# Counting sixteen of 128 edge tiles ahead of the first projection of a graph network, with one-hots from GpSimd and ScalarE

## The chip, the cores and the metric

The kernel runs on one core of a Trainium2 chip. The metric is the device time of one execution in microseconds (us), the median of several runs. Engine names are those of the profile: PE is TensorE's matmul, PEld its weight load, DVE is VectorE, ACT is ScalarE, POOL is GpSimd, SP is SyncE, which here only issues DMAs.

## What is computed

A graph network over 1024 nodes of 512 features and 16384 edges. The rows of x are normalised and cut at zero, normalised again over the nodes (a batch norm), and go through a graph convolution; four layers of cross attention and a gated feed-forward follow, and a second graph convolution. Cut to what matters here:

```python
h = max(layernorm(x), 0)
h = batchnorm(h) ; h = gcn(h, src, dst, gcn_in_w)
for i in range(4): h += attention(ln(h), cond) ; h += feed_forward(ln(h))
h = gcn(h, src, dst, gcn_out_w) ; return x + h + h0
# gcn: out[d] = sum over edges (s, d) of (h @ W)[s] * dinv[s] * dinv[d] + b, with self loops
```

A graph convolution is done as a product with a dense matrix of counts: how many edges run from source s to target d. The change concerns how that matrix is built, once, in the opening of the kernel. The targets are sorted.

## The kernel before

**Order.** The kernel is written as one program. A scheduler places each engine's instructions by their dependencies and by the order of the program text; `tc.issue_after(x)` keeps what is issued under it behind x in that order, and `waiting_for(x, engine)` (L82) makes each instruction of one engine wait for x. Each engine works its own queue strictly in order.

**The opening, to 27 us.** SP and ACT issue the loads of the edges (L333, L334), of x in eight blocks (L338), of two groups of `cond`, and of weights. POOL makes the identity, issues seven small loads of parameters (`prow`, `grow`, L356 to L362), casts the identity to bf16 (L484) and numbers the nodes 0 to 1023 in f32 (`ids_f`, L346). DVE splits each edge's source into a low part (0 to 127) and a high part and combines the high part with the target's offset in its window into one key (L370 to L383). PE turns both so that an edge tile is a column (L393), ACT copies them out (`edges_t`, L401; `minus_low`, L404), then PE turns the parameters (`pc`, `pg`, L397 and L399) and ACT copies those (L409, L410). ACT also casts the numbers to f16 (`ids`, L411). PE turns four blocks of `cond` (L184 `tr_cond`, copied by ACT at L244), then the eight blocks of x that DVE has normalised (statistics L151 and L152, root L134 to L143, scaling L172; transposes L184 `tr_x`; ACT cuts at zero into `h0T`, L431). DVE takes the batch statistics of `h0T` (L437, L439), works out the root and the scale and shift (L134 to L143, L443 to L445, the last being `bshift`), and DVE and ACT apply them (L450, L453). Meanwhile PE turns four more blocks of `cond` and makes the first key products (`pa_kT`, L301), in two halves with an ACT copy between (`firsts`, L322).

**The counting loop, 27 to 79 us.** The 16384 edges are 128 tiles of 128 edges. Because the targets are sorted, a tile's edges fall in a window of 48 targets (`WIN`). For tile t, `count(t)` makes two one-hot matrices, `low` (edge by low part, 128x128) and `hot` (edge by high part and window offset, 128x384), and PE multiplies them into PSUM (`cs`, L537); a finished half block gets the identity added (L534), is copied by ACT (L541), and is summed by DVE into degrees (`degrees`, L491). `hot` is always made by DVE (L524). `low` is made by DVE for four tiles of each eight (L502), and by ACT for the other four (`low_hots`, L505: four Abs, one Relu). Into this loop the 32 steps of the first projection (`hw_in`, L461, a step being one 128x512 product that the profile records as two matmuls) are woven, one for each four tiles (L626 to L629), by a generator. `low` has 5 buffers, `hot` 10, `off` 2. PSUM has 8 banks in turn (`bank`, L92).

**After it**: the first value product, the last degrees, a branch for unsorted inputs that is not taken (L637), the root of the degrees, the aggregation (L655), and the four layers.

Of the kernel before, what the change touches and what calls it, by code (L numbers as in the profile page):

```python
# [10 lines left out]
BF16 = mybir.dt.bfloat16  # L11
F32R = mybir.dt.float32r
I32 = mybir.dt.int32
AF = mybir.ActivationFunctionType
OP = mybir.AluOpType
AX = mybir.AxisListType

P = 128
# [5 lines left out]
def gnn_kernel(  # L24
# [26 lines left out]
    nc = tc.nc  # L51

    N, D = x.shape
# [6 lines left out]
    NB = N // P  # L60
    KC = D // P
    HP = H // 2
    ET = E // P
# [17 lines left out]
    @contextmanager  # L81
    def waiting_for(ins, engine):  # L82

        traced = nc.cur_bb.bb.instructions
        n = len(traced)
        yield
        for i in traced[n:]:
            if i.engine == engine:
                tc.add_manual_dep(i, ins.ins.name, mybir.DependencyInfo(
                    mybir.DependencyClass.Sync, mybir.DependencyReason.DATA))  # L90

    def bank(name):  # L92
        return psum.tile([P, 512], F32, tag="bank", name=name)

    def t512(name, dtype=F32):
        return work.tile([P, 512], dtype, tag="t512", name=name)

    def slot(name):
        return slots.tile([P, 2, 512], F32, tag="slot", name=name)

    def slots_of(n, name):
        return [slot(f"{name}_{i}") for i in range(n)]
# [17 lines left out]
    def four(t):  # L120
        return t.rearrange("p (a b) -> p a b", a=4)
# [67 lines left out]
    ident = const.tile([P, P], F32, name="ident")  # L189
    make_identity(nc, ident)  # L190
    ones = const.tile([P, 1], F32, name="ones")
# [40 lines left out]
    def turn_cond(g, by=(0, 1)):  # L232

        t = slots_of(4, f"ct_0_{g}")
        tiles = raw_conds.pop(g)
        for i, ctile in enumerate(tiles):
            pt = transposed(ctile, f"cond_{g}_{i}")
            r0 = (i % MB) * P
            to = t[i // MB].rearrange("p a (b c) -> p a b c", b=2)[:, :, :, r0:r0 + P]
            of = pt.rearrange("p (a b c) -> p a b c", a=2, b=2)  # L240
            if by[i % 2]:
                nc.vector.tensor_copy(to, of)
            else:
                nc.scalar.copy(to, of)  # L244
        return t
# [91 lines left out]
    for nb in range(NB):  # L337
# [4 lines left out]
    w_in = load_w(gcn_in_w, "w_in")  # L342
    raw_wv = load_w(Wv[0], "wv_0")

    ids_f = slot("ids_f").rearrange("p a b -> p (a b)")
    numbered = nc.gpsimd.iota(ids_f, pattern=[[1, N]], base=0, channel_multiplier=0,  # L346
                   allow_small_or_imprecise_dtypes=True)
    ids = gp.tile([P, N], F16, name="ids")
    tid = gp.tile([P, 1], I32, name="tid")
    nc.gpsimd.iota(tid, pattern=[[0, 1]], base=0, channel_multiplier=1)  # L350

# [14 lines left out]
    WIN = 48  # L366
# [26 lines left out]
        nc.tensor.transpose(pe[:, i * P:(i + 1) * P], edges_f[:, i, :], ident)  # L393
    pout = bank("outside")
    nc.tensor.matmul(pout[:1, :2], ones, outside, start=True, stop=True)
    pc = bank("pc")
    nc.tensor.transpose(pc[:, :n_cols], prow, ident[:n_cols, :n_cols])  # L397
    pg = bank("pg")
    nc.tensor.transpose(pg[:, :P], grow, ident)  # L399
    edges_t = gp.tile([P, 2, ET], F32, name="edges_t")  # L400
    nc.scalar.copy(edges_t, pe[:, :2 * P].rearrange("p (a b) -> p a b", a=2))  # L401
    low_t, key_t = edges_t[:, 0, :], edges_t[:, 1, :]
# [3 lines left out]
    nc.vector.tensor_copy(n_out, pout[:1, :2])  # L406
    total_out = gp.tile([1, 1], I32, name="total_out")
    nc.vector.tensor_tensor(total_out, n_out[:, 0:1], n_out[:, 1:2], OP.add)
    nc.scalar.copy(cols, pc[:, :n_cols])  # L409
    nc.scalar.copy(gcols, pg[:, :P])  # L410
    ids_made = nc.scalar.copy(ids, ids_f)  # L411
    (_, load_act, load_pe, load_dve, _), (unsorted,) = nc.values_load_multi_w_load_instructions(total_out, min_val=0,
                                                                   max_val=2 * P)

    with tc.issue_after(load_pe.ins), tc.issue_after(load_act.ins):
        turned = [turn_cond(0, (0, 0))]
    cond_turned = transposed.last


# [5 lines left out]
    for nb, xn in enumerate(scaled(xb, mean, root, "x", xb)):  # L425
        with tc.issue_after(cond_turned.ins):
            pt = transposed(xn, f"x{nb}")
        c0 = (nb % 4) * P
        for k in range(2):
            with tc.issue_after(ids_made.ins):  # L430
                nc.scalar.activation(h0T[nb // 4][k][:, :, c0:c0 + P],  # L431
                                     four(pt)[:, 2 * k:2 * k + 2, :], AF.Relu)
    bmv = small.tile([P, KC, 2], F32, tag="bmv", name="bmv", bufs=1)
    bst = small.tile([P, KC, 2, 6], F32, tag="bst", name="bst", bufs=1)
    for i in range(2):
# [35 lines left out]
    def rows_of(name):  # L471
        pairs = slots_of(NB // 2, name)
        return [pairs[nb // 2][:, nb % 2, :] for nb in range(NB)]

    def by_sources(t):
        return t.rearrange("p a (s n) -> p (a s) n", n=P)

    C = slots_of(NB, "c")
    counts = [by_sources(c.bitcast(F32R)) for c in C]
    ident_16 = gp.tile([P, P], BF16, name="ident_16")
    nc.gpsimd.tensor_copy(ident_16, ident)  # L484
    sums = slot("sums")
    sums_t = sums.rearrange("p a b -> p (a b)")
    pdeg = bank("deg")

    HALF = P // 2

    def degrees(d, of, part):  # L491

        nc.vector.tensor_tensor(part, of[:, 0, :], of[:, 1, :], OP.add)
        nc.vector.tensor_tensor(part[:, :2 * P], part[:, :2 * P], part[:, 2 * P:], OP.add)
        of_d = sums_t[:, d * P:(d + 1) * P]
        nc.vector.tensor_tensor(of_d, part[:, :P], part[:, P:2 * P], OP.add)
        nc.tensor.matmul(pdeg[:, d:d + 1], of_d, ones, start=True, stop=True,
                         skip_group_check=True)

    def low_hot(t, name):  # L500
        hot = gp.tile([P, P], BF16, tag="low", name=name, bufs=5)
        nc.vector.tensor_scalar(hot, ids[:, :P], low_t[:, t:t + 1], None, OP.is_equal)  # L502
        return hot

    def low_hots(t, n):  # L505

        off = gp.tile([P, n, P], BF16, tag="off", name=f"off_{t}", bufs=2)
        for i in range(n):
            nc.scalar.activation(off[:, i, :], ids[:, :P], AF.Abs, bias=minus_low[:, t + i:t + i + 1])
        nc.scalar.activation(off, off, AF.Relu, bias=1.0, scale=-1.0)  # L510
        return [off[:, i, :] for i in range(n)]

    acc, counted, lows = {}, {}, {}

    def touched(t):
        f = first_of[t]
        return range(f // HALF, (f + WIN - 1) // HALF + 1)

    def count(t):
        if t % 8 == 0:  # L520
            lows.update(zip(range(t + 4, t + 8), low_hots(t + 4, 4)))
        low = lows.pop(t) if t in lows else low_hot(t, f"lo_{t}")
        hot = gp.tile([P, NB, WIN], BF16, tag="hot", name=f"hot_{t}", bufs=10)
        nc.vector.tensor_scalar(hot.rearrange("p s n -> p (s n)"), ids[:, :NB * WIN],  # L524
                                key_t[:, t:t + 1], None, OP.is_equal)
        for j in touched(t):
            begun = j in acc
            if not begun:
                acc[j] = bank(f"cs_{j}")
            done = t + 1 == ET or j not in touched(t + 1)  # L530
            n0, n1 = max(first_of[t], j * HALF), min(first_of[t] + WIN, (j + 1) * HALF)
            to = acc[j].rearrange("p (s n) -> p s n", n=HALF)
            if done:
                nc.tensor.matmul(to[:, j // 2, :], ident_16,  # L534
                                 ident_16[:, j % 2 * HALF:(j % 2 + 1) * HALF],
                                 start=False, stop=False, skip_group_check=True)
            nc.tensor.matmul(to[:, :, n0 - j * HALF:n1 - j * HALF],  # L537
                             low, hot[:, :, n0 - first_of[t]:n1 - first_of[t]],
                             start=not begun, stop=done, skip_group_check=True)
            if done:  # L540
                nc.scalar.copy(counts[j // 2][:, :, j % 2 * HALF:(j % 2 + 1) * HALF], to)  # L541
                counted[j] = t
        for j, when in list(counted.items()):
            if t - when >= 8:
                if j % 2:
                    degrees(j // 2, C[j // 2], t512(f"part_{j // 2}"))
                del counted[j]

    def count_any():

# [47 lines left out]
    def add_left(left, parts, to, root, name):  # L598

        for d in range(NB):  # L600
            nc.sync.dma_start(left.rearrange("p a b -> p (a b)"), left_dram[d])
            pl = bank(f"left_{name}_{d}")
            for s in range(NB):
# [11 lines left out]
             for step in project_steps(nb, h0T, w_in, "in",  # L615
# [4 lines left out]
    conds[0, 1] = cond_blocks(turned[1])  # L620
    begun = {"k0": begin(0, 0, "kT", of_k(blocks_of_w(raw_wk), conds[0, 0]), firsts[:, 0, :],
                         shifted_last)}
    with ExitStack() as behind:
        for begun_by in (scaled_last, shifted_last):
            behind.enter_context(tc.issue_after(begun_by.ins))
        for t in range(ET):  # L626
            if t % (ET // (NB * KC)) == 0:
                next(steps)
            count(t)  # L629
        for _ in steps:  # L630
            pass
        begun["v0"] = begin(0, 0, "v", of_v(blocks_of_w(raw_wv), conds[0, 0]), firsts[:, 1, :])
        with tc.issue_after(load_dve.ins):
            for j in counted:
                if j % 2:
                    degrees(j // 2, C[j // 2], t512(f"part_{j // 2}"))
# [735 lines left out]
```

## Time and profile before

| what | us |
|---|---|
| median of 3 runs (2533.81 to 2534.73) | 2534.37 |
| the profiled execution | 2532.89 |
| its span, first to last instruction | 2531.1 |
| PE busy in the span | 2506.6 |
| DVE, ACT, POOL busy | 1403.6, 557.3, 646.0 |
| start of the first projection step | 26.67 |
| start of the first value product, behind the counting loop | 78.74 |

The page gives busy time by engine, the same in 40 slices, DMA, the chain of work that ended last, and groups of instructions. The timeline gives instructions in order: start, duration, engine, line, operation, output and inputs, shape, and in brackets how long the engine had idled and for whom. A duration includes the latency of the operation; what one of several costs in a row is read from the distance of their starts. The granted clock of PE is 1.000 over the span.

### The profile page before, as it was taken

The page shows a single profiled execution, that of the slowest core. Times are in us where ns is not written, and L with a number is a line of the kernel's source. Part 1 is how long each engine was busy: PE and PEld are TensorE (multiplying, and loading weights), DVE is VectorE, ACT ScalarE, POOL GpSimd, SP SyncE. Part 2 cuts the span into 40 slices and gives each one's busy share as a digit, 9 for nine tenths or more (in the row PEclk, how much of TensorE's full clock was granted, in tenths as well). Part 3 has the DMA queues.
Part 4 walks back from the last instruction along what each step waited for, and adds up shares of the span by engine and source line. Part 5 has one row for each costly group of instructions (what it writes and reads, how often), then busy time and mean ns, then how long its engine had stood idle before and what let it go on. Part 6 is the DMA issues. An engine that isn't in the chain of part 4 may idle for free. (4 is left out here: it accounts for less than half of the span.)

```text
span 2531.1 us, 32228 instructions
## 1 busy us (share of the span) xinstructions
PE 2506.6 (99%) x12464; PEld 1768.6 (70%) x12464; DVE 1403.6 (55%) x3026; ACT 557.3 (22%) x1318; POOL 646.0 (26%) x539
## 2 busy tenths in 40 slices
PE   8999999999999999999999999999999999999999
PEld 5778886666578887655587888556676888566565
DVE  9655566544574556544474556644484455654551
ACT  7322222111122223111122222111112222211111
POOL 0322224532210003533320003253320002352410
PEclk9999999999999999999999999999999999999999
DMA  5302232111122112010211212110112121111020
GB/s 179 131 31 91 92 128 64 38 50 35 61 64 70 46 59 76 26 54 17 96 38 67 72 63 67 34 55 17 59 67 64 53 78 60 44 34 64 11 88 34
DMA packets 67136, 156.81 MB, mean 62 GB/s; under 512 B 5576, under 2 KB 5904, under 8 KB 66976
## 3 DMA queue, kind: packets, MB, share of 16 engines
q1 hardware_dynamic: 64880, 149.25, 17.8%
q0 software_dynamic: 1376, 4.30, 0.5%
q8 instruction: 103, 1.69, 0.3%
q10 hardware_dynamic: 720, 1.11, 0.1%
q14 instruction: 57, 0.47, 0.1%
HBM read 133.66 MB, written 20.97 MB: 61 GB/s over the span
## 5 line engine op out<-in xcount | busy, mean ns | idle before, releaser
L301 PE MATMUL ga<-ln3T,wval 128*128 128x512 f32 x512 | 233.9, 593 | 0.0
L932 ACT ACTIVATE g<-g,gcols 128x512 f32<-128x512 f32 x128 | 92.4, 722 | 430.9 <-DVE g L945 366.3
L301 PEld LDWEIGHTS ga<-ln3T,wval 128*128 128x128 f32 x512 | 96.0, 190 | 109.9 <-issue 109.0
L776 ACT ACTIVATE pr<-sc,nmax 128x256 f32<-128x256 f32 x256 | 118.0, 473 | 176.8 <-DVE nmax L771 176.8
L847 POOL TENSOR_TENSOR os<-oT 128x256 f32<-128x256 f32 x12 | 8.7, 726 | 566.9 <-DVE oT L822 566.9
L1006 POOL TENSOR_TENSOR hall<-fu,hall 128x512 f32<-128x512 f32 x24 | 30.4, 1269 | 429.0 <-DVE fu L1005 429.0
L301 PE MATMUL pa_v<-wv,ct 128*128 128x256 f32 x512 | 123.1, 379 | 0.0
L301 PE MATMUL fa<-wff,fT 128*128 128x256 f32 x512 | 121.6, 379 | 0.0
L301 PE MATMUL gc<-ln3S,wgate 128*128 128x512 f32 x256 | 120.4, 593 | 1.1 <-DVE gu L942 1.1
L301 PE MATMUL pc_v<-wv,ct 128*128 128x256 f32 x512 | 121.0, 379 | 0.0
L301 PE MATMUL pd_v<-wvs,ct 128*128 128x256 f32 x512 | 121.0, 379 | 0.0
L301 PE MATMUL pd_k<-ct,wks 128*128 128x256 f32 x512 | 121.0, 379 | 0.0
L301 PE MATMUL pc_k<-ct,wk 128*128 128x256 f32 x512 | 120.9, 379 | 0.0
L301 PE MATMUL gd<-ln3T,ges 128*128 128x512 f32 x256 | 120.6, 593 | 0.0
L301 PE MATMUL gb<-ln3S,ges 128*128 128x512 f32 x256 | 120.3, 592 | 0.0
L301 PE MATMUL gc<-ln3T,wgate 128*128 128x512 f32 x256 | 120.3, 592 | 0.0
L301 PE MATMUL gd<-ln3S,ges 128*128 128x512 f32 x256 | 120.3, 592 | 0.0
L301 PE MATMUL pa_k<-ct,wk 128*128 128x256 f32 x480 | 116.2, 385 | 0.0
L301 PEld LDWEIGHTS fa<-wff,fT 128*128 128x128 f32 x512 | 97.3, 190 | 21.7 <-issue 9.6
L301 PEld LDWEIGHTS pd_k<-ct,wks 128*128 128x128 f32 x512 | 97.3, 190 | 13.2
L301 PEld LDWEIGHTS pd_v<-wvs,ct 128*128 128x128 f32 x512 | 97.3, 190 | 13.2
L301 PEld LDWEIGHTS pc_k<-ct,wk 128*128 128x128 f32 x512 | 97.3, 190 | 13.2
(318 smaller groups left out, 4883.5 us busy)
## 6 DMA issues: line engine op xcount, KB each, us to landing
ct<-cond_dram SPq DMA_DIRECT2D x72, 512.0 KB, 4.5
wval<-in_L_gnn_geglu_w_dram SPq DMA_DIRECT2D x32, 512.0 KB, 3.6
wgate<-in_L_gnn_geglu_w_dram SPq DMA_DIRECT2D x32, 512.0 KB, 4.6
wff<-in_L_gnn_ffo_w_dram SPq DMA_DIRECT2D x32, 512.0 KB, 4.6
cond_dram<-ct SPq DMA_DIRECT2D x24, 512.0 KB, 3.2
cond<-in_L_gnn_cond_dram SPq DMA_DIRECT2D x32, 256.0 KB, 4.4
ct<-cond_dram SPq DMA_DIRECT2D x24, 256.0 KB, 4.5
wk<-in_L_gnn_Wk_dram SPq DMA_DIRECT2D x8, 512.0 KB, 5.3
```

The costliest lines, as they stand in the source:

```text
L301: nc.tensor.matmul(at, left[:, k, l0:l1], right[:, k, r0:r1], start=start and n == 0 and k == 0, stop=n == len(cols_of) - 1 and k == 1, sk ...
L776: nc.scalar.activation(pr3[:, a, :], ps3[:, a, :], AF.Exp, bias=nmax[:, a:a + 1], accum_out=tot[:, a:a + 1])
L847: t.tensor_tensor(s1, a21, a22, OP.add)
L932: nc.scalar.activation(pre, pre, AF.Gelu, bias=gcols[:, cg:cg + 1])
L1006: t.tensor_tensor(h21, halves_of(u2), h21, OP.add)
```

## The change

The numbering is made by GpSimd in f16 directly, without the f32 copy and ScalarE's cast. The functions of the counting are moved up, unchanged but for an argument that names the engine. Tiles 0 to 3 are counted ahead of the transposes of the first `cond` group, tiles 4 to 7 behind them, tiles 8 to 15 between the two halves of the opening key product and behind it. For tiles 0 to 7 `low` comes from ScalarE and `hot` from GpSimd; for tiles 8 to 15 both come from GpSimd, each instruction waiting for the end of DVE's scaling of x. `pc`, `pg` and their copies move behind tile 7. The loop keeps its 128 turns and its projection steps, but counts only from tile 16 on, so that the first four steps follow each other.

On GpSimd the numbering now stands ahead of the making of the identity and of the seven DMA issues. On PE the order becomes: edge transposes, tiles 0 to 3, `tr_cond`, tiles 4 to 7, `pc`, `pg`, `tr_x`, the second `tr_cond`, the first half of `pa_kT`, tiles 8 to 11, its second half, tiles 12 to 15, and five projection steps before the matmuls of tile 16. On GpSimd the last three `low` of tiles 13 to 15 stand behind all the `hot`.

```diff
-    ids_f = slot("ids_f").rearrange("p a b -> p (a b)")
-    numbered = nc.gpsimd.iota(ids_f, pattern=[[1, N]], base=0, channel_multiplier=0,
-                   allow_small_or_imprecise_dtypes=True)
     ids = gp.tile([P, N], F16, name="ids")
+    numbered = nc.gpsimd.iota(ids, pattern=[[1, N]], base=0, channel_multiplier=0,
+                              allow_small_or_imprecise_dtypes=True)
...
-    pc = bank("pc")
-    nc.tensor.transpose(pc[:, :n_cols], prow, ident[:n_cols, :n_cols])
-    pg = bank("pg")
-    nc.tensor.transpose(pg[:, :P], grow, ident)
...
+    EARLY = 16
...
+    def low_hot(t, name, by=nc.vector):
+        hot = gp.tile([P, P], BF16, tag="low", name=name, bufs=5)
+        by.tensor_scalar(hot, ids[:, :P], low_t[:, t:t + 1], None, OP.is_equal)
+        return hot
...
+    def count(t, by=nc.vector):
+        if t % 8 == 0 and t >= EARLY:
+            lows.update(zip(range(t + 4, t + 8), low_hots(t + 4, 4)))
+        low = lows.pop(t) if t in lows else low_hot(t, f"lo_{t}", by)
+        hot = gp.tile([P, NB, WIN], BF16, tag="hot", name=f"hot_{t}", bufs=10)
+        by.tensor_scalar(hot.rearrange("p s n -> p (s n)"), ids[:, :NB * WIN],
+                         key_t[:, t:t + 1], None, OP.is_equal)
...
+    for t in (0, 4):
+        lows.update(zip(range(t, t + 4), low_hots(t, 4)))
+    for t in range(4):
+        count(t, nc.gpsimd)
...
+    with tc.issue_after(load_pe.ins), tc.issue_after(load_act.ins):
+        turned = [turn_cond(0, (0, 0))]
+    for t in range(4, 8):
+        count(t, nc.gpsimd)
+    pc = bank("pc")
+    nc.tensor.transpose(pc[:, :n_cols], prow, ident[:n_cols, :n_cols])
+    pg = bank("pg")
+    nc.tensor.transpose(pg[:, :P], grow, ident)
     nc.scalar.copy(cols, pc[:, :n_cols])
     nc.scalar.copy(gcols, pg[:, :P])
-    ids_made = nc.scalar.copy(ids, ids_f)
...
         for k in range(2):
-            with tc.issue_after(ids_made.ins):
-                nc.scalar.activation(h0T[nb // 4][k][:, :, c0:c0 + P],
-                                     four(pt)[:, 2 * k:2 * k + 2, :], AF.Relu)
+            nc.scalar.activation(h0T[nb // 4][k][:, :, c0:c0 + P],
+                                 four(pt)[:, 2 * k:2 * k + 2, :], AF.Relu)
...
+    with waiting_for(scaled.last, mybir.EngineType.Pool):
+        for t in range(8, EARLY):
+            count(t, nc.gpsimd)
...
         for t in range(ET):
             if t % (ET // (NB * KC)) == 0:
                 next(steps)
-            count(t)
+            if t >= EARLY:
+                count(t)
```

More of the change, by code (lines that the diff above doesn't have):

```diff
@@ L408, in gnn_kernel, with by_sources @@
     nc.vector.tensor_tensor(total_out, n_out[:, 0:1], n_out[:, 1:2], OP.add)
-    nc.scalar.copy(cols, pc[:, :n_cols])
-    nc.scalar.copy(gcols, pg[:, :P])
-    ids_made = nc.scalar.copy(ids, ids_f)
+    def by_sources(t):
+        return t.rearrange("p a (s n) -> p (a s) n", n=P)
+    C = slots_of(NB, "c")
+    counts = [by_sources(c.bitcast(F32R)) for c in C]
+    ident_16 = gp.tile([P, P], BF16, name="ident_16")
+    nc.gpsimd.tensor_copy(ident_16, ident)
+    sums = slot("sums")
+    sums_t = sums.rearrange("p a b -> p (a b)")
@@ new lines, in gnn_kernel, with degrees @@
+    pdeg = bank("deg")
+    HALF = P // 2
+    EARLY = 16
+    def degrees(d, of, part):
+        nc.vector.tensor_tensor(part, of[:, 0, :], of[:, 1, :], OP.add)
+        nc.vector.tensor_tensor(part[:, :2 * P], part[:, :2 * P], part[:, 2 * P:], OP.add)
+        of_d = sums_t[:, d * P:(d + 1) * P]
+        nc.vector.tensor_tensor(of_d, part[:, :P], part[:, P:2 * P], OP.add)
+        nc.tensor.matmul(pdeg[:, d:d + 1], of_d, ones, start=True, stop=True,
+                         skip_group_check=True)
@@ new lines, in low_hot, with low_hots @@
+    def low_hot(t, name, by=nc.vector):
+        hot = gp.tile([P, P], BF16, tag="low", name=name, bufs=5)
+        by.tensor_scalar(hot, ids[:, :P], low_t[:, t:t + 1], None, OP.is_equal)
+        return hot
+    def low_hots(t, n):
+        off = gp.tile([P, n, P], BF16, tag="off", name=f"off_{t}", bufs=2)
+        for i in range(n):
+            nc.scalar.activation(off[:, i, :], ids[:, :P], AF.Abs, bias=minus_low[:, t + i:t + i + 1])
+        nc.scalar.activation(off, off, AF.Relu, bias=1.0, scale=-1.0)
+        return [off[:, i, :] for i in range(n)]
@@ new lines, in gnn_kernel, with touched @@
+    acc, counted, lows = {}, {}, {}
+    def touched(t):
+        f = first_of[t]
+        return range(f // HALF, (f + WIN - 1) // HALF + 1)
+    def count(t, by=nc.vector):
[5 more added lines that the diff above has]
+                         key_t[:, t:t + 1], None, OP.is_equal)
+        for j in touched(t):
+            begun = j in acc
+            if not begun:
+                acc[j] = bank(f"cs_{j}")
+            done = t + 1 == ET or j not in touched(t + 1)
+            n0, n1 = max(first_of[t], j * HALF), min(first_of[t] + WIN, (j + 1) * HALF)
+            to = acc[j].rearrange("p (s n) -> p s n", n=HALF)
+            if done:
+                nc.tensor.matmul(to[:, j // 2, :], ident_16,
+                                 ident_16[:, j % 2 * HALF:(j % 2 + 1) * HALF],
+                                 start=False, stop=False, skip_group_check=True)
+            nc.tensor.matmul(to[:, :, n0 - j * HALF:n1 - j * HALF],
+                             low, hot[:, :, n0 - first_of[t]:n1 - first_of[t]],
+                             start=not begun, stop=done, skip_group_check=True)
+            if done:
+                nc.scalar.copy(counts[j // 2][:, :, j % 2 * HALF:(j % 2 + 1) * HALF], to)
+                counted[j] = t
+        for j, when in list(counted.items()):
+            if t - when >= 8:
+                if j % 2:
+                    degrees(j // 2, C[j // 2], t512(f"part_{j // 2}"))
+                del counted[j]
@@ L416, in gnn_kernel @@
         turned = [turn_cond(0, (0, 0))]
+    for t in range(4, 8):
[4 more added lines that the diff above has]
+    nc.tensor.transpose(pg[:, :P], grow, ident)
+    nc.scalar.copy(cols, pc[:, :n_cols])
+    nc.scalar.copy(gcols, pg[:, :P])
     cond_turned = transposed.last
@@ L473, in rows_of @@
         return [pairs[nb // 2][:, nb % 2, :] for nb in range(NB)]
[L478 to L547, printed above, removed]
```

## The prediction, made before the changed kernel was run

> **What bounds the kernel now.** I read the table of engines, the 40 slices, the table by stage, then the timeline of the opening engine by engine. The chain that ended last is no help: it goes back only 1% of the span. PE and DVE in the slices (each digit is a fortieth of the span, 63 us):
>
> ```profile
> PE   8999999999999999999999999999999999999999
> DVE  9655566544574556544474556644484455654551
> ```
>
> PE has air only in the first slice; after it the kernel is a stream of PE work, so what the change shortens ahead of it shifts the rest. That slice by stages (width, then busy time and count of PE, PEld, DVE, ACT, POOL, clock, DMA share, GB/s):
>
> ```profile
> 0.00:10.00 10.00, 1.04 (x4) 0.45 (x4) 6.50 (x29) 1.83 (x3) 5.77 (x16) 1.00 0.82 276
> 20.00:30.00 10.00, 7.63 (x33) 4.77 (x32) 9.48 (x39) 6.96 (x15) 0.00 (x0) 1.00 0.98 249
> ...
> 49.50:55.88 6.38, 6.38 (x42) 3.71 (x41) 6.20 (x28) 5.34 (x13) 0.00 (x0) 1.00 0.00 0
> ```
>
> Two stages with two limits. To 27 us DVE carries the chain: statistics of x, its root (11.44 to 13.66), the scaling (13.66 to 17.40), statistics of `h0T` (17.77 to 22.6), a second root from 22.97, `bshift` at 25.7; PE waits. POOL is free from 6.5. In the counting loop the row 49.50:55.88 is one period of 16 tiles and four projection steps: PE 6.38 of 6.38, DVE 6.20. PE is the bound, by little. PE at the loop's start:
>
> ```profile
> 26.67 1.98 PE L461 MATMUL hw_in<-w_in,h0T 128*128 128x512 f32 x4 [1.69 <-ACT h0T L453]
> ...
> 31.25 0.84 PE L537 MATMUL cs<-hot,off 128*128 128x384 bf16 x7 [0.23 <-ACT off L510]
> ...
> 33.84 1.06 PE L461 MATMUL hw_in<-w_in,h0T 128*128 128x512 f32 x2
> ```
>
> The reader is to see two marks: the first step starts at 26.67, and the fifth, tile 16's, at 33.84, **7.17 us** later. From the fifth on, both kernels give PE the same sequence.
>
> **The change part by part.** *The loop.* Between the two marks the changed kernel has four steps and nothing else. Two matmul records, one step, take 0.86 (the pair at 35.44 is followed at 36.30): 4 x 0.86 = 3.44. Gain 7.17 - 3.44 = **3.73**. Of it 4 x 0.67 = 2.7 is matmuls (a group of four tiles takes 0.67, 42.68 to 43.35), the rest is waits for the first one-hots. After the mark DVE starts tile 16 when the scaling of `h0T` ends, about 0.9 behind step 1, hence 2.5 us ahead of PE; with PE at 6.38 a period against DVE's 6.20, I take no further gain and no loss. If ACT's first `off` group comes late (it now stands behind two copies and behind `hs_in`, which waits for step 4), PE waits some 0.3.
>
> *The delay of the first step.* PE's `tr_cond` ends at 14.50 (the first `tr_x` starts at 14.52). Now 0.67 for tiles 4 to 7, 0.24 for `pc` (10.29 to 10.53) and about 0.13 for `pg` stand before `tr_x`: start 15.5, first block turned at 16.1, ACT's `cols` and `gcols` done by 16.1 as well, so `h0T` starts at 16.15 where it had started at 15.62. The removed cast of 1.05 us (13.54 on ACT) is what keeps this small. **Plus 0.53** on DVE's chain, which waits for ACT at 17.77 (0.37 idle). Tiles 0 to 3 cost nothing: ACT's ten operations (eight of about 0.31, two of about 0.55: 3.6) fill 6.76 to 10.4, PE is idle until the first `cond` block at 11.05, and ACT until 12.20. The moved numbering (1.02) delays identity and parameter loads by about 1 us; the identity is wanted at 3.73, the parameters now only at 15.4.
>
> *GpSimd's one-hots.* No compare of this kind stands in the trace. Near it stand a row of the timeline and two groups by form (busy, mean ns):
>
> ```profile
> 5.26 0.30 POOL L484 CAST ident<-ident 128x128 bf16<-128x128 f32 x1
> ```
>
> ```profile
> L1279 POOL TENSOR_TENSOR hall<-hall,ffb 128x512 f32<-128x512 f32 x32 | 39.5, 1265 | 0.6
> ...
> L849 POOL TENSOR_TENSOR os<-os,oT 128x256 f32<-128x256 f32 x12 | 9.0, 749 | 0.0
> ```
>
> With one input or none: 0.30 for 128 columns, 1.02 for the 1024 of the numbering, so 0.51 for a `hot` of 384 and 0.30 for a `low`. With two inputs: 0.2 + 0.0021 a column, so 1.0 and 0.45. A compare against a column of scalars reads one tile, so I take 0.51 and 0.30 and keep 1.0 and 0.45 as the upper end. Tiles 0 to 7 then run from 6.6 (`edges_t` at 6.58) to 10.7, before anything waits; tiles 8 to 15 from 17.4 to 17.4 + 8 x 0.81 = 23.9, and PE wants the last of them before 27.2. [...]
>
> *What GpSimd does to DVE.* Two neighbours at 716 us:
>
> ```profile
> 715.97 1.26 POOL L837 TENSOR_TENSOR wos<-wo,wo 128x512 f32<-128x512 f32 x1
> 716.07 1.19 DVE L139 SCALAR_TENSOR_TENSOR a_ln<-y_ln,v_ln 128x2 f32<-128x2 f32 x1
> ...
> 718.51 0.16 DVE L143 SCALAR_TENSOR_TENSOR y_ln<-b_ln,y_ln 128x2 f32<-128x2 f32 x1
> ```
>
> A root's operation of 0.16 us takes 1.19 and ends with POOL's. So while POOL runs back to back, each two-input operation of DVE's root costs one POOL operation instead of 0.2. The statistics are free of it (L151 is at most 0.70 everywhere). Behind the delayed operation stand the rest of the root, `bshift`, ACT's shift and PE's first step. With 0.51 and 0.30, POOL ends at 23.9 and the second root begins at 22.97 + 0.53 = 23.5: one or two operations, **plus 0.3**.
>
> **Sum**: -3.73 + 0.53 + 0.3 = **-2.9**. The profiled execution, 2532.89, becomes 2530.0; it lies 1.48 below the median of the runs shown, so the median becomes 2534.37 - 2.9 = **2531.5**. A measurement of this kernel tells about 0.2%, 5.07 us, from no change; the forecast lies inside. Its own range, for 0.3 us of `off` and 1 us of overlap either way, is 2529.8 to 2533.
>
> **Rivals.** *The port eats the gain* (0.17). If `hot` is over 0.6 us, tiles 0 to 7 are still running when x's root begins at 11.44, and tiles 8 to 15 cover the whole second root. [...] At 1.0 and 0.45: 14.6 and 2.3 late; 19.7 to 31.3; `bshift` at 32.1 instead of 25.7: -3.73 + 6.4 = +2.7, 2537.1. For it: the row at 716. Against: cast and numbering at 0.8 ns a column.
>
> *GpSimd's compare is slow outright* (0.15), the rival on the other side. Same place; it decides from about 1.15 us a `hot`. At 1.2 and 0.55: first eight end at 16.2, x's root 3.7 late; the second eight run from 21.1 to 35.1, `bshift` at 35.7, 10 late: +6.3, 2540.7, slower by 0.25%; every 0.1 us more adds about 1.7. For it: no compare in the trace bounds it. Against: it would be slower than two-input adds.
>
> *More than forecast* (0.12). PE is slow when it starts (two answers by tile; min, median and max in ns):
>
> ```profile
> L184 PE MATMUL tr_cond<-ident,cond x16: 421/421/447, 11.1 to 14.3; 128*128 128x128 f32 x16
> ```
>
> ```profile
> L184 PE MATMUL tr_x<-ident,x x32: 272/273/422, 14.5 to 18.6; 128*128 128x128 f32 x32
> ```
>
> Sixteen transposes take 3.4 us at 421 ns each; the second set takes 1.75 (18.67 to 20.41). If PE is at pace by 11 us because tiles 0 to 3 ran at 9, `tr_cond` ends 0.7 earlier (the `cond` blocks, 256 KB at about 390 GB/s, land every 0.67) and the 0.53 goes; DVE's L383, which lasts 0.99 until the cast ends, may end 0.4 earlier; PE free of waits would need about 0.1 less in each of 7 periods. Together -3.73 - 0.4 - 0.7 = -4.8, 2529.6; past -5.07 something unseen must help, which I give 0.08 of the 0.12. [...]
>
> *The change doesn't shorten the loop*, because DVE, not PE, sets its pace from the start: between 27.57 and 43.16 DVE is busy all 15.59. But DVE loses 16 tiles too, 8 x 0.39 + 8 x 0.23 = 5.0 us, more than PE's 3.73. I give it nothing of its own.
>
> **How the numbers follow.** Forecast 0.56, port 0.17, slow compare 0.15, more 0.12. Same: 0.56 + 0.17 + 0.04 = 0.77; faster 0.08; slower 0.15. The range runs from 2529.3, just past the better case's -4.8, to 2541, past the two-input price and into the slow compare up to about 1.2 us: some 0.08 is left below it and 0.10 above.
>
> **What would show it.** The first step at 27.2 to 27.6 and the fifth 3.4 later, near 30.9; the value product at 75.8 instead of 78.74. POOL's L455 (`hot`) near 0.5; if near 1.0, L139 to L143 stretch to that in both roots. `tr_x` at 15.5. A period of the loop other than 6.38, or a later stage that does not shift with the opening, would make it wrong.

## The result, and the profile after

Over 11 runs of each the changed kernel takes 2539.97 us (2538.95 to 2541.69), the kernel before 2533.81: a ratio of 1.0024, with an interval of 1.0017 to 1.0032. It is **slower by 6.2 us**, where I had forecast 2.9 faster. The profiled execution has a span of 2537.4 us, 6.3 more than before.

PE in the 40 slices of the changed kernel:

```profile
PE   7999999999999999999999999999999999999999
```

PE's first digit has gone from 8 to 7: work was to be moved into the air of this slice, and there is more air. The rest is the stream of before. By stages, in the columns of before, with the same period of the loop, which now lies 5.7 later:

```profile
20.00:30.00 10.00, 7.64 (x44) 6.48 (x43) 9.48 (x27) 5.11 (x14) 10.00 (x12) 0.85 1.03 232
55.20:61.58 6.38, 6.38 (x43) 3.71 (x41) 6.20 (x28) 5.35 (x13) 0.00 (x0) 1.00 0.00 1
```

The period is untouched (PE 6.38, DVE 6.20). What is new stands in two columns of the first row: GpSimd busy 10.00 of 10.00, where it had 0.00, and a granted clock of 0.85. PE around the start of the loop:

```profile
27.29 3.44 PE L301 MATMUL pa_kT<-ct,wk 128*128 128x256 f32 x8
33.40 0.34 PE L468 MATMUL cs<-hot,lo 128*128 128x352 bf16 x2 [2.51 <-POOL lo L433]
33.98 1.11 PE L468 MATMUL cs<-hot,lo 128*128 128x288 bf16 x4 [0.24 <-POOL lo L433]
34.89 5.67 PE L540 MATMUL hw_in<-w_in,h0T 128*128 128x512 f32 x10
```

The first step starts at 34.89 (26.67 before): 8.22 late. Ahead of it PE stands at tile 13 and waits 2.51 for GpSimd's `lo`, and the steps, which stand behind it in PE's queue, wait too. The fifth step starts at 39.54 (33.84 before), the value product at 84.17 (78.74). From there on each VectorE instruction, counted from the end in both traces, lies 6.06 to 6.30 later, but for differences that pass again. So the loss is made in the first 95 us. GpSimd's new groups, by form (busy, mean ns of one):

```profile
L455 POOL TENSOR_SCALAR hot<-ids,edges_t 128x384 bf16<-128x384 f16 x16 | 20.0, 1262 | 0.0
L433 POOL TENSOR_SCALAR lo<-ids,edges_t 128x128 bf16<-128x128 f16 x8 | 4.8, 610 | 3.2 <-DVE x L172 3.2
```

I had put in 0.51 and 0.30. At these prices the first eight run from 6.30 to 16.11, beside x's root, and the second eight from 19.74 to 34.53, beside the second root. x's root on DVE:

```profile
11.21 0.60 DVE L134 TENSOR_SCALAR v_x<-x_mean 128x8 f32<-128x8 f32 x1
11.85 0.63 DVE L136 TENSOR_SCALAR y_x<-v_x 128x8 int32<-128x8 int32 x1
12.51 0.52 DVE L139 SCALAR_TENSOR_TENSOR a_x<-y_x,v_x 128x8 f32<-128x8 f32 x1
13.06 0.17 DVE L141 TENSOR_TENSOR b_x<-a_x,y_x 128x8 f32<-128x8 f32 x1
```

Each took 0.17 before; the two later L139 take 0.78 each. The root ends at 15.91 instead of 13.66. While four of GpSimd's `hot` run (11.21 to 16.11), five of the root's eleven operations are held up; the other six keep their 0.17. The second root ends (`bshift`) at 29.33 instead of 25.70. ACT's shift of `h0T`, for which the first step waits, follows:

```profile
29.43 2.93 ACT L532 ACTIVATE h0T<-h0T,bshift,bscale 128x512 f32<-128x512 f32 x4 [4.84 <-DVE bshift L524]
```

The first of these four ends at 30.24. So the data of the first step was there at about 30.3, and PE still started it only at 34.89.

### The profile page after: what moved, and what is told of

The parts are those of the page before. It is cut to its first block, busy times and chain, and to the rows that moved or that the text cites. A ratio compares the mean times of both kernels' runs of the same rounds, so it can differ in the third digit from the quotient of the medians.

```text
span 2537.4 us, 32227 instructions
## 1 busy us (share of the span) xinstructions
PE 2512.0 (99%) x12464; PEld 1770.6 (70%) x12464; DVE 1406.5 (55%) x3002; ACT 557.6 (22%) x1317; POOL 671.3 (26%) x563
## 5 line engine op out<-in xcount | busy, mean ns | idle before, releaser
L1015 POOL TENSOR_TENSOR hall<-fu,hall 128x512 f32<-128x512 f32 x24 | 30.4, 1268 | 428.9 <-DVE fu L1014 428.9
```

The costliest lines, as they stand in the source:

```text
L1015: t.tensor_tensor(h21, halves_of(u2), h21, OP.add)
```

## Experiments

My theory after the result: the price of GpSimd's compare was mis-sized, and it acts in two ways, by holding up DVE's roots and by holding up PE, which counts GpSimd's last tiles before its first step. The first is called the port below, as in the prediction; what the traces show of it is that some of DVE's operations take longer while GpSimd runs (L139 0.52 and 0.78, 0.17 before), not the path itself. Rivals: the port alone, PE's order alone, and other terms of my sum being wrong as well. In what follows, "opening" is the shift of the VectorE instructions at 110 us against before in the profile: it is sharper than the medians, to which later stages add events of 1.2 to 1.7 us (last section). Each opening comes from one profiled execution. Medians are set against the kernel before as measured beside each run (2533.21 to 2533.42).

### What makes the compare slow: forms

Edit: in the last stage, behind the last `into_parts`, groups of two or three of such GpSimd operations, 384 columns each (slices of the tiles left out here):

```diff
+nc.gpsimd.tensor_scalar(o16, i16, key, None, OP.is_equal)
+nc.gpsimd.tensor_scalar(o16, i16, key, None, OP.subtract)
+nc.gpsimd.tensor_scalar(o16, i16, 3.0, None, OP.is_equal)
+nc.gpsimd.tensor_copy(o16, i16)
...
```

> The kernel before, with operations of GpSimd added in the last stage whose results nothing reads; each covers 384 columns. Its time is not what is asked; the durations of its GpSimd rows are. Three theories of why a one-hot took 1.22 to 1.25 us where a cast of 128 columns took 0.30. (1) The compare itself is slow: the four forms with is_equal (16-bit or 32-bit, against a column of scalars or a constant) take about 1.2, and subtract, multiply, add and the copies about 0.5 or less. (2) The column of scalars makes it slow: is_equal, subtract and multiply against the column take about 1.2, is_equal and add against a constant about 0.5. (3) The 16-bit operands make it slow: everything from f16 or into bf16 takes about 1.2, the copy and the cast too, and is_equal of f32 into f32 about 0.5.

The groups by form:

```profile
L1346 POOL TENSOR_SCALAR o<-i,dinv 128x384 bf16<-128x384 f16 x3 | 3.7, 1239 | 0.0
L1350 POOL TENSOR_SCALAR o<-i,dinv 128x384 bf16<-128x384 f16 x3 | 3.7, 1238 | 0.0
L1352 POOL TENSOR_SCALAR o<-i 128x384 bf16<-128x384 f16 x3 | 3.4, 1159 | 0.0
L1354 POOL TENSOR_SCALAR o<-i 128x384 f32<-128x384 f32 x2 | 2.3, 1166 | 0.0
L1360 POOL CAST o<-i 128x384 bf16<-128x384 f32 x3 | 1.4, 497 | 0.0
```

L1346 is `is_equal` against the column, L1350 `subtract`, L1352 `is_equal` against a constant, L1354 an `add` of a constant in 32 bits, L1360 a cast (the copies in 16 and 32 bits took the same). **None of the three theories holds.** In these probes each operation with a scalar took 1.16 to 1.24 (`is_equal`, `subtract`, `add`, `multiply`; f16 into bf16, f32 into f32); copies and casts took 0.50. `is_equal` against the column took 0.08 more than against the constant (1.239 and 1.159). From the changed kernel's `lo` (128 columns, 0.610) to its `hot` (384, 1.262) it is 2.5 ns a column.

### Was the price all? copies

Edit, for GpSimd's tiles alone, and likewise for `lo` (shortened):

```diff
-by.tensor_scalar(hot, ids[:, :NB * WIN], key_t[:, t:t + 1], None, OP.is_equal)
+by.tensor_copy(hot, ids[:, :NB * WIN])
```

> The changed kernel in which GpSimd casts the numbering into the one-hot tiles (a copy without a scalar) in place of each compare: the counts of tiles 0 to 15 are not the reference's. Everything else, order, waits, sizes and DMAs, is that of the change. The probes took 0.50 us for such a cast of 384 columns, which is the 0.51 that my prediction had put in for the compare. Theory, only that price was mis-sized: the first eight end near 10.5, x's root takes its old 2.2 us, the second eight end near 24, the first step starts at 27.2 to 27.6, the fifth 3.4 later, the value product near 75.8, and the kernel is 2.9 us faster than before (between 1.5 and 3.9). Rival, other terms were wrong as well (the delay behind tiles 4 to 7, PE's waits for one-hots, a gain that the loop gives back): the first step after 28 or the value product after 77.2, and less than 1.5 us gained.

2530.62 us against 2533.42, **2.8 us faster** (0.999, 0.9981 to 0.9999); opening -2.88. GpSimd's `hot` (the `lo` took 0.29) and PE's first steps:

```profile
L459 POOL CAST hot<-ids 128x384 bf16<-128x384 f16 x16 | 7.5, 503 | 0.0
```

```profile
27.87 4.56 PE L546 MATMUL hw_in<-w_in,h0T 128*128 128x512 f32 x10 [1.56 <-ACT h0T L538]
```

PE waits for ACT's `h0T` again, not for GpSimd. First step 27.87 (0.3 later than forecast), fifth 31.40, value product 76.04 (75.8 forecast). With the price that I had assumed, the total that I had forecast comes out, so the price is what turned a gain into a loss. That it comes out to 0.1 us is partly luck, since the first step's delay of 1.20 is not made up as I had it (0.53 behind tiles 4 to 7, 0.3 from the port). One other operation of DVE, the sum of two single numbers, took 1.63 beside GpSimd's casts, against 0.13 before (L408):

```profile
6.91 1.63 DVE L403 TENSOR_TENSOR total_out<-n_out 1x1 int32<-1x1 f32 x1
```

By it x's root ended at 14.98, 1.32 late, with all its operations at 0.17, and PE stood ready for x's transposes (0.57 idle, start 15.68). Of this 0.87 reached the statistics of `h0T`; the second root added 0.33, in its first operation. At the fifth step the gain was 2.44, not 2.9, and the loop and what follows it gave 0.44 more, for which I had put nothing.

### The port and PE's order: late, port_reads, port_writes

`late` leaves GpSimd's sixteen `hot` where they are and takes tiles 8 to 15 out of PE's way (`make_hot` is the compare of `count` by itself; PE counts these tiles in the loop). Their eight `low` go back to DVE and ACT, so GpSimd's second set is lighter and ends at 29.43 instead of 34.53:

```diff
-    EARLY = 16
+    EARLY = 8
...
-        for t in range(8, EARLY):
-            count(t, nc.gpsimd)
+        for t in range(8, 16):
+            hots[t] = make_hot(t, nc.gpsimd)
```

> The changed kernel in which GpSimd still makes all sixteen hots at the same two places, but PE counts tiles 8 to 15 in the loop, behind the first two steps (their lows come from DVE and ACT, as before). The port stays, the wait of PE in order goes. Theory: bshift ends near 29.3 and the first step starts near 30.2, as in the sum of the two root delays (2.25 of x's root, of which 1.8 reaches the second, and 1.7 to 1.9 of the second); the fifth step follows 3.44 and 8 x 0.17 later, near 35.0 where the changed kernel had 39.54: 1.7 us slower than before (1.0 to 2.9), not 6.2. Rival, the port alone makes the 8.2 us of delay: first step near 34.9 still, some 7 us slower.

```profile
29.94 4.54 PE L544 MATMUL hw_in<-w_in,h0T 128*128 128x512 f32 x6 [3.28 <-ACT h0T L536]
```

The first step comes at 29.94, near the 30.2 of the theory; the rival had 34.9. So of the 8.22 of delay the **port makes 3.27 and PE's order 4.95**, by this run. Since the `low` are missing from GpSimd here, it understates the port: `bshift` ends at 28.98, against 29.33 in the changed kernel, whose own trace has the step's data ready at about 30.3, which makes the split 3.6 and 4.6. The whole is 2537.44, 4.0 slower (1.0014, 1.0005 to 1.0023), above the 1.0 to 2.9 that I had expected. PE ran at half clock from 30.5 to 33.9 (the first three steps took 4.54, 2.84 in `late_params`), so the fifth step came at 36.77 and not near 35.0; the opening is +2.59, and later stages add 0.8 in the profile.

`port_reads` puts the same compares into the kernel before, where nothing uses them, all into one buffer (tiles 8 to 15, `lo` and `hot`, likewise behind the scaling of x):

```diff
+    for t in range(8):
+        nc.gpsimd.tensor_scalar(unread, ids[:, :384], key_t[:, t:t + 1], None, OP.is_equal)
```

> The kernel before, in which DVE and ACT still make every one-hot and PE counts all tiles in the loop; GpSimd makes the same sixteen compares at the same two places, and nothing reads them (the numbering is written in 16 bits at once, as in the changed kernel). What delayed the first step from 26.67 to 34.89 is split by it. Theory, half port and half PE's order: x's root ends near 15.9 (13.66 before), the second root's bshift near 29.3 (25.7), the first step starts near 30.2, and the kernel is 3.2 to 3.9 us slower than before. Rival, all of it is PE waiting in order for GpSimd's last tiles: no delay here, first step at 26.7, time as before within 0.5 us. Rival, all of it is the port: first step near 34.9, slower by some 8 us.

2540.07, 6.84 slower (1.0026, 1.0017 to 1.0035): too much for my theory, and by another way. The roots are less delayed than in the changed kernel (x's ends at 14.21, `bshift` at 27.48, first step 28.45). Here the compares lie further apart (the first eight span 10.88, 9.81 in the changed kernel), and all write one buffer. But GpSimd runs on until 36, and DVE, which here makes the first one-hots of the loop beside it, takes 0.42 to 0.58 for some of them (0.31 otherwise). PE also ran at half clock from 28.0 to 31.4, so that the first two steps took 3.46 (1.98 before). The fifth step comes 2.9 late; no run parts these two causes. A second half clock at 89.5 adds 1.0, and the opening is +4.90. The slower one-hots are a third way that the changed kernel does not take, since DVE's first sixteen tiles are gone there. So this run does not split the delay; `late` does.

`port_writes` replaces the compares by numberings:

> As port_reads, but GpSimd's unread operations at the two places are numberings, which write and read nothing: 1024 columns (about 1.0 us) for a hot, 512 for a low. It asks what in a compare delays DVE. Theory, its reads: DVE's two-input operations (L139, L141, L143 of both roots) keep their 0.17, and x's root ends within 0.9 us of 13.66; the first step starts at 26.7 to 27.6, slower by 0 to 1 us. Rival, any GpSimd operation does it: these lines stretch to 0.4 to 0.8 as in the changed kernel, bshift near 27.5, the first step near 28.4, slower by some 5 to 7 us as port_reads was.

2540.27, 6.85 slower (1.0026, 1.0016 to 1.0035). The theory holds for the lines that it named and fails for the time. DVE's groups in the first 40 us:

```profile
L460 DVE TENSOR_SCALAR h0T<-h0T,bscale,bshift 128x512 f32<-128x512 f32 x4 | 3.9, 1028 | 0.0
L136 DVE TENSOR_SCALAR y_bn<-v_bn 128x4 int32<-128x4 int32 x1 | 1.0, 1020 | 0.0
L139 DVE SCALAR_TENSOR_TENSOR a_x<-y_x,v_x 128x8 f32<-128x8 f32 x3 | 0.5, 167 | 0.1
```

The two-input operations of DVE's roots (L139, L141, L143) kept their 0.16 to 0.17 beside GpSimd's numberings. Its one-input operations with scalars (L136, 1.02, 0.17 before; the scaling of `h0T`, 1.03, 0.54 before; the first `lo` and `hot` of the loop, 1.02 and 0.96, where 0.25 and 0.31 are usual) were held up beside the numberings too. My prediction had only the first kind on its list. The time of this run is not the port's alone: the first step comes 1.54 late, and from there PE ran at half clock for two stretches in a row (29.4 to 36.3; the pair of a step took 1.91 and 1.53 there, 1.02 to 1.06 behind it), so that the fifth, at 39.21, comes 5.37 late.

### How many tiles: early8, early4

```diff
-    EARLY = 16
+    EARLY = 8
```

`early4` has 4 there, and the two loops that count tiles 4 to 7 and 8 to 15 early are left out.

> The changed kernel with only tiles 0 to 7 counted early, so that GpSimd has no second set. Theory: GpSimd still ends at 16.1 and x's root is still 2.2 us late, which reaches the second root as 1.8; the second root is then undisturbed and takes its old 2.7 us, the first step starts near 28.5, PE finds it without a wait on GpSimd, and the loop gives back 8 tiles x 0.17 = 1.34 and some 0.5 to 1 of waits for the first one-hots: -0.3 us against before, between -0.9 and +0.3. Rival, the loss goes with the number of tiles: half of +6.2, +3.1 us.

> The changed kernel with only tiles 0 to 3 counted early (ACT makes the lows of 4 to 7 early as well). Theory: GpSimd ends at 11.2, just as x's root begins, which takes its old 2.2 us; the condition transposes start some 0.7 late (11.8), since PE waits for the fourth hot until 11.28, and pc and pg stand ahead of the x transposes; the first step starts between 27.4 and 27.8 (26.67 before); the loop gives back 4 x 0.17 = 0.67 and 0.2 to 0.5 of waits: 0.0 us against before, between -0.5 and +0.5. Rival, the loss goes with the number of tiles: +1.5 us.

`early8`: first step 28.42 (28.5 expected), no wait on GpSimd, value product 78.72 (78.74 before). The loss does not go with the number of tiles: half of the value product's 5.43 would have been 2.7. The opening is +0.40. The whole is +1.65 (1.0004, 0.9995 to 1.0013), above the -0.9 to +0.3 expected, and by itself too wide to rule out the rival's +3.1; in the profile +0.4 and +1.7 of it are two stretches of half clock, at 86.1 and 2373.1. `early4`: first step 27.90, value product 78.42, whole -1.05 (0.9995, 0.9986 to 1.0004): below the -0.5 to +0.5 expected, but not to be told from before.

### The half clock: warm

In the profile of the changed kernel, the table by stage around two waits of PE (clock in the third column from the end):

```profile
27.00:30.40 3.40, 3.38 (x9) 2.69 (x9) 3.15 (x9) 0.97 (x2) 3.40 (x4) 0.50 1.03 144
33.80:37.20 3.40, 3.11 (x7) 1.48 (x8) 2.54 (x11) 0.10 (x1) 0.74 (x2) 0.51 1.02 360
```

The first stretch of 0.50 falls on the key product (3.44 for eight records, 1.99 in `late`) and is hidden behind GpSimd; the second falls on the four steps, 4.65 instead of 3.44. `warm` keeps PE busy in its waits:

```diff
+            for _ in range({10: 3, 11: 6, 12: 5, 13: 12, 14: 2, 15: 1}.get(t, 0)):
+                nc.tensor.matmul(pdeg[:, P:2 * P], ident, ident, start=True, stop=True,
+                                 skip_group_check=True)
             count(t, nc.gpsimd)
```

> The changed kernel with matmuls of 128 columns, whose results nothing reads, put into PE's waits for GpSimd's tiles 10 to 15, so that PE does not stand idle there. In the profile of the changed kernel the granted clock is 0.50 for 3.4 us from 27.0 and again from 33.8, both behind such waits, and the four steps took 4.65 us (34.89 to 39.54) where two records a step of 0.43 make 3.44. Theory, the idle waits bring the half clock: it does not come at 33.8, the first step still starts near 34.9 (GpSimd's last low sets it), the fifth at 38.3, and the kernel is some 1.2 us faster than the changed kernel, 5 us slower than before (4.3 to 5.7). Rival, the half clock does not hang on the waits: it comes as it did, and the time stays at +6.2. If the added matmuls run at half clock themselves they end after GpSimd's tiles and the first step comes up to 2 us later.

```profile
27.00:30.40 3.40, 3.40 (x32) 3.38 (x32) 3.15 (x9) 1.06 (x2) 3.40 (x4) 1.00 1.06 158
33.80:37.20 3.40, 3.26 (x16) 1.84 (x15) 1.98 (x10) 2.91 (x9) 0.95 (x2) 1.00 0.98 383
```

Full clock throughout; first step 34.98, fifth 38.46 (1.08 earlier), 2538.31 us, 5.1 slower than before (1.0022, 1.0012 to 1.0032). So in the changed kernel PE's idle waits bring the half clock, at some 1.1 us. The other executions point the same way: the granted clock over the whole span is 0.997 to 0.999 in all eleven of the changed kernel, and 0.999 or 1.000 in eight of the nine of `warm` (0.998 in the ninth).

### A version that avoids both: free_windows, late_params

GpSimd makes four hots before x's root and four beside the statistics of `h0T`; PE counts the eight tiles between the halves of the key product (`EARLY` is 8, and `pc`, `pg` and their copies stand where the kernel before has them):

```diff
+    for t in range(4):
+        hots[t] = make_hot(t, nc.gpsimd)
...
     with waiting_for(scaled.last, mybir.EngineType.Pool):
-        for t in range(8, EARLY):
-            count(t, nc.gpsimd)
+        for t in range(4, 8):
+            hots[t] = make_hot(t, nc.gpsimd)
+    for t in range(8):
+        count(t)
```

> Tiles 0 to 7 alone are moved, and GpSimd's compares lie where DVE has no small operation with two inputs and no scaling: four hots from 6.3 to 11.2, before x's root, and four from 17.4 to 22.3, beside the statistics of h0T; ACT makes the eight lows early; PE counts the eight tiles between the halves of the key product, in its idle time ahead of the first step; pc and pg stay where they were. Theory: x's root ends at 13.7 and bshift at 25.7 as before, the first step starts at 26.7 (26.4 to 27.2), the loop gives back 8 x 0.17 = 1.34 and 0.2 to 1 us of waits: value product at 76.4 to 77.2 (78.74 before), 1.5 to 2.3 us faster than before. Rival, GpSimd delays DVE whatever DVE does: the statistics grow beyond 0.70 us each, bshift comes after 27, nothing gained.

2533.98, +0.56 (1.0001, 0.9992 to 1.001). The statistics stay at 0.66 to 0.69, both roots at 0.16 to 0.17 an operation: compares in these places delay nothing on DVE. But the condition transposes started at 11.44 and the first step at 27.42; the opening gained 1.36, and the value product came at 77.72, not at 76.4 to 77.2. `late_params` also moves `pc`, `pg` and their copies behind the x transposes:

> As free_windows (tiles 0 to 7 early, GpSimd's compares beside x's and h0T's statistics), with pc and pg and their two copies behind the x transposes. In the profile of free_windows the condition transposes started at 11.44 (11.08 before), behind pg, whose parameters land a microsecond later since the numbering is ahead of their DMAs, and the first step at 27.42 (26.67 before). Theory: that goes; first step at 26.7 (26.4 to 27.2), fifth at 32.1 (33.84 before), value product near 77.0; the opening is 2.1 us shorter than before (free_windows: 1.36). On the whole time 2.1 us faster, or 0.6 where GpSimd's and DVE's order on their port falls the other way once in a later layer, as it did in the profile of free_windows at 1610 (+1.5). Rival, something later gives it back whole: 0 or slower.

```profile
26.51 2.84 PE L542 MATMUL hw_in<-w_in,h0T 128*128 128x512 f32 x6 [1.04 <-ACT h0T L534]
```

First step 26.51, fifth 31.96, value product 76.82, 1.92 ahead of before. **2530.95 us, 2.3 faster than before** (0.999, 0.9981 to 0.9999), the only kernel here with the reference's counts whose interval lies below 1. Its two executions with a granted clock of 0.999 over the span took 2532.67 (the profiled one) and 2532.29, the nine with 1.000 took 2530.67 to 2531.25.

## Why the prediction was wrong

**The step that failed** is the price: "A compare against a column of scalars reads one tile, so I take 0.51 and 0.30." It measured 1.23 to 1.26 and 0.61. Going by the inputs was wrong: the cast's pace was right for a cast (0.503 in `copies`), but the probes with a scalar took 1.16 to 1.24, with a column or a constant. I had kept the two-input rows as the upper end, and the price lies above even that (1.0).

**The loop's gain, 3.73**, was right: in `warm` the four steps take 3.48 (3.44 in the sum), in `copies` 3.54. **The delay of 0.53 and the port's 0.3** are not borne out term by term: in `copies` the first step came 1.20 late, 0.87 of it by `total_out`, an operation that I had not listed, and 0.33 by the second root. That -2.9 measured -2.8 there is right in the price and partly luck in the rest.

**The rival "GpSimd's compare is slow outright"** gave +6.3 at 1.2 and 0.55; the kernel measured +6.16. Its first eight end at 16.11 (16.2 predicted), its second at 34.53 (35.1). But its mechanism was half wrong: it had `bshift` at 35.7 and measured 29.33, because not each two-input operation of DVE was held up, but 3 of the 9 in x's root and 4 of the 12 in the second. What held the first step to 34.89 was PE in order behind GpSimd's last `lo`. I had written that "PE wants the last of them before 27.2" and did not carry this wait to the slow price. Both lead to GpSimd's end, so the sizes are near. That they agree to 0.2 us is luck: the rival had no half clock in it, and without one (`warm`) the loss is 5.1. The port rival's sum at 1.0 and 0.45, +2.7, has the first eight end at 14.6, x's root 2.3 late, and the second eight run from 19.7 to 31.3; the changed kernel has 16.11, 2.25 late, and 19.74 to 34.53.

**The sum as measured**, at the fifth step, with the split of `late`: 3.27 port + 4.95 PE's order + 1.21 half clock - 3.73 gain = +5.70, which is 39.54 - 33.84. The loop takes back 0.27 (value product +5.43), a half clock at 91.9 adds 0.6, and 0.2 more comes by 716 us: +6.3 in the profiles.

**The clock** I had weighed only for a gain (0.7 in the better case, for `tr_cond` at pace earlier), never for a loss. The gain did not come: the sixteen `tr_cond` took 3.65, as before. In the trace of the changed kernel each stretch of half clock in the opening lasts 3.41 us, twice that in `port_writes`. Ahead of the first PE waited 0.9 and 1.5 us, ahead of the second 2.5; with these waits filled (`warm`) neither came.

**What held**: the place of the x transposes behind tiles 4 to 7 (not their start: 16.83, and 15.68 in `copies`, where I had 15.5), the period of 6.38, DVE no bound of its own, and the range, whose upper end (2541) was drawn by this rival.

## What to carry to other kernels

Price an operation on another engine by a row of the same instruction form on that engine (here: 1.16 to 1.24 with a scalar, 0.50 for a copy), not by the number of tiles that it reads; where there is no such row, a probe of a few idle operations settles it in one run. Before giving GpSimd work beside a chain of small VectorE operations, find the stretches where VectorE does statistics or waits, and put it there: in `free_windows` the statistics stayed at 0.66 to 0.69 and the roots at 0.16 to 0.17 an operation. And early work must not stand in an engine's queue ahead of its critical work unless that early work is surely done: here that order cost 4.95 of the first step's 8.22 us.

## What the runs showed of the hardware

**Half clock after the same wait, or not.** The same wait of 1.89 us, in the kernel before and in `early8`, by PE's timeline:

```profile
2372.39 1.56 PE L301 MATMUL fd<-wffs,fs 128*128 128x256 f32 x6 [1.89 <-DVE fs L978]
2373.78 1.89 PE L301 MATMUL fb<-wffs,fs 128*128 128x256 f32 x8
```

```profile
2372.80 2.71 PE L301 MATMUL fd<-wffs,fs 128*128 128x256 f32 x6 [1.89 <-DVE fs L987]
2375.30 2.47 PE L301 MATMUL fb<-wffs,fs 128*128 128x256 f32 x8
```

In the second the granted clock is 0.50 for 3.4 us, and 1.7 us are lost for good. The kernel before also met it once, in the execution of `forms` (27.0 to 30.4), and not in its own profile. In the trace of the changed kernel the clock changes at 27.02, 30.43, 33.84, 37.26, 91.87, 95.28 and 2535.81, whole multiples of 3.413 us apart. The half clock of `early8` runs from 2373.06 to 2376.47, and its wait lies whole in the 3.41 ahead of that (2369.64 to 2373.06). In the kernel before the one change is at 2531.47, just behind its last instruction; counted back from it in the same steps, a border at 2371.04 divides the wait. Cut that way from 17 us on, the traces of these two, before and changed, have five full-clock stretches in which PE idled for 2.12 to 3.41 us by its records, each followed by half clock; the next below them, 1.90 in the changed kernel at 2375.39, was not, and the one with 1.89 in `early8` was. What decides near 1.9 stays open. Such a stretch is one source of scatter between runs of one kernel, and of medians that differ from the opening by a microsecond.

**Who starts first.** The feed-forward at 1610 us, before and in `free_windows`:

```profile
1610.30 0.74 DVE L955 TENSOR_TENSOR fT<-gv,g 128x512 f32<-128x512 f32 x1
1610.44 1.73 POOL L212 TENSOR_TENSOR wffs<-wff 128x512 f32<-128x512 f32 x1
```

```profile
1609.87 1.27 POOL L212 TENSOR_TENSOR wffs<-wff 128x512 f32<-128x512 f32 x1
1610.08 1.62 DVE L968 TENSOR_TENSOR fT<-gv,g 128x512 f32<-128x512 f32 x1 [0.44 <-DVE gv L966]
```

Here the one that starts first keeps its pace (DVE 0.74, GpSimd 1.27), and the other is stretched by 0.46 (GpSimd, 1.73) or 0.88 (DVE, 1.62); with GpSimd first, DVE is 0.58 ahead of before at `gv` (L966) and 0.66 behind at its next `fT` (L969), a loss of 1.24. It fell that way once each in `free_windows` and `port_writes` (there at 444 us: GpSimd 1.26, DVE 1.60, 0.73 before). What tips it, 0.14 us between the two starts, stays open.
